# Layer 3's band matrices, stored with the tile index innermost

## The chip, the cores and the metric

The kernel runs on one core of a Trainium2 chip. The metric is the time of one execution on the device, in microseconds (us). A core has TensorE (PE, matrix products; its weight loads are listed apart as PEld), VectorE (DVE), ScalarE (ACT), GpSimd (POOL) and SyncE (SP, which issues the transfers here). SBUF is the on-chip working memory, PSUM the memory that TensorE writes its results to.

## The reference

Four layers act on an input of 16 images of 64 x 64 places and 256 channels, each as `x = x + layer(groupnorm(x))`. The change touches the last one, an involution: a convolution whose 7 x 7 kernel is made anew for each place, from the reduced channels there, and shared by the 16 channels of a group.

```python
def _L3_conv_ref(x, w_reduce, gamma, beta, mean, var, w_span, b_span):
    K = 7; G = 16
    B, H, W, C = x.shape
    r = jnp.einsum('bhwc,cd->bhwd', x, w_reduce)
    r = jax.nn.relu((r - mean) * (gamma / jnp.sqrt(var + BN_EPS)) + beta)
    kgen = jnp.einsum('bhwd,de->bhwe', r, w_span) + b_span
    kgen = kgen.reshape(B, H, W, G, K * K)
    ...
    patches = patches.reshape(B, H, W, K * K, G, Cg)
    out = jnp.einsum('bhwgk,bhwkgc->bhwgc', kgen, patches)
    return out.reshape(B, H, W, C)
```

All numbers are fp32.

## The kernel before

Layers 0 to 2 run first, in stages of their own; layer 3 is the last stage of the program.

Layer 3 cuts a 64 x 64 image into 22 x 8 tiles of 3 rows by 8 columns (`TR`, `TC`; 176 tiles, `NTL`), so a tile has 24 output places (`TILE_OUT`). The places that a tile's outputs look at form a window of 9 x 14 = 126 inputs (`TILE_IN`). For one tile and one group of 16 channels the involution is then one product: the 126 inputs, as rows, times a banded matrix of 126 x 24 that holds the generated kernels at the right rows. The channels are the columns of the stationary operand, the 24 outputs those of the moving one.

`reduced` (L1332) makes the reduced channels `rt` of an image, in a layout by the place within a tile and then by tile (L1360 the products, L1367 their way out of PSUM).

`matrices` (L1375) makes the band matrices of a quarter of the channels (64 channels, 4 groups) of an image. It fills two tiles of memory `w` (name `wm`), one for each pair of groups, `q`. A step `n` makes four output places: for each of them one product (L1393) of the `span` weights, moved by the place's offset within the window, with the 176 tiles' `rt` columns. The results, 4 x 176 floats in each of 128 rows, lie in the PSUM tile `pk`, two places to a bank. They are copied to `wm` with the bias `spanb` added: in 5 of 12 steps by four instructions of ScalarE (L1403, 176 floats each), in 7 of 12 by one of VectorE (L1408, 704 floats). The copy's target is `dst` (L1400). PSUM tiles `pk` are taken from three buffers, so TensorE can be three steps ahead of the copies.

In `wm` the 48 outputs of a pair of groups lie side by side for a tile, and the tiles follow each other: shape [128, 176, 48]. A step's copy writes for each of its four places 176 floats that are 48 floats apart.

`involution7` (L1450) uses them. A turn is two rows of tiles (`k` = 0, 1, eleven tile rows apart) of one quarter of one image: for 8 tile columns `tj`, 2 `k` and 2 `q`, 32 products (L1459). The stationary operand is the window of 32 channels of a pair of groups, from `xw`; the moving operand is that tile's 48 floats of `wm[q]`. The four products of one `tj` write to four different sets of 32 PSUM partitions of `pa`, and so use four column groups of the array. Each product has two instructions in the profile (45,056 for 704 turns). Both of a pair's groups are computed for all of its 32 channels; ScalarE (L1469) and VectorE (L1470) pick the right one by a mask, and POOL (L1477) adds the residual `rx`.

The order is written out by hand, in the loop over `turns` (L1501): 16 images x 4 quarters x 11 turns. In each turn the loads for turns ahead are issued on SP (`xw` four turns ahead, out of six buffers; `rx` two), then `involution7`, then 2 or 3 steps of `matrices` for the quarter that follows (`STEPS`, 24 steps in 11 turns), then now and then a part of `reduced` for the next image. The matrices of the very first quarter are made before the first turn. `wm` has four buffers: two for the quarter in use, two for the one that is being made.

Of the kernel before, what the change touches and what calls it, by code (L numbers as in the profile page):

```python
# [9 lines left out]
F32 = mybir.dt.float32  # L10
# [5 lines left out]
P = 128  # L16
# [13 lines left out]
NTR, NTC = 22, HW // TC  # L30
TILE_IN = (TR + 6) * (TC + 6)
TILE_OUT = TR * TC
# [12 lines left out]
def network(ctx: ExitStack, tc: tile.TileContext, a: dict, out: bass.AP):  # L45
# [139 lines left out]
    with ExitStack() as st:  # L185
# [399 lines left out]
        for n in range(LAST + 16):  # L585
            m, t = divmod(n, NCH)
# [64 lines left out]
    with ExitStack() as st:  # L651
# [24 lines left out]
        with tc.tile_pool(name="s_conv", bufs=1) as pcv:  # L676
# [8 lines left out]
            for dj in range(7):  # L685
                dst = band if dj == 0 else term
# [22 lines left out]
        for n in range(10):  # L709
# [4 lines left out]
                rhs=maps[:, c, :, delta : delta + NB],  # L714
# [5 lines left out]
        m = maps[:, 0, :, 2 : 2 + NB]  # L720
# [18 lines left out]
        with tc.manual_schedule():  # L739
# [25 lines left out]
            for n, (ch, g) in enumerate(steps):  # L765
# [18 lines left out]
                b, k = g * 8, min(8, NI - g * 8)  # L784
# [8 lines left out]
        n = NI * NCH  # L793
# [505 lines left out]
    with ExitStack() as st:  # L1299
        pc = st.enter_context(tc.tile_pool(name="c_const", bufs=1))  # L1300
        wk = st.enter_context(tc.tile_pool(name="c_work", bufs=2))
        wm_p = st.enter_context(tc.tile_pool(name="c_wm", bufs=4))
# [70 lines left out]
        NTL = NTR * NTC  # L1373

        def matrices(i, quarter):  # L1375


            rto = rts[i % 2].rearrange("k a b t u -> k (a b) (t u)")
            wms[i, quarter] = wm = []
            for q in range(2):  # L1380
                w = wm_p.tile([P, NTL, 2 * TILE_OUT], F32, tag="wm", name="wm")
                wm.append(w)
                first = quarter * 4 + q * 2
                for n in range(12):

                    pk = wg.tile([P, 2, CT], F32, tag="wg", name="pk")
                    pkv = pk[:, :, 0 : 2 * NTL].rearrange("p b (m t) -> p b m t", m=2)
                    for m in range(2):
                        for b in range(2):
                            gg, o = divmod(n * 4 + b * 2 + m, TILE_OUT)  # L1390
                            s0 = SPAN - P - (o // TC * (TC + 6) + o % TC)
                            half = slice(b * 64, b * 64 + 64)
                            nc.tensor.matmul(  # L1393
                                pkv[:, b, m],
                                lhsT=span[half, first + gg, s0 : s0 + P],
                                rhs=rto[half, o // 4 * 2 + m, :],
                                start=True, stop=True,
                            )
                    g0 = first * TILE_OUT + n * 4
                    dst = w[:, :, n * 4 : n * 4 + 4].rearrange("p t (b m) -> p b m t", b=2)  # L1400
                    if (q * 12 + n) % 12 in (1, 3, 6, 8, 11):
                        for m in range(4):
                            nc.scalar.activation(  # L1403
                                dst[:, m // 2, m % 2], pkv[:, m // 2, m % 2], AF.Identity,
                                bias=spanb[:, g0 + m : g0 + m + 1],
                            )
                    else:
                        nc.vector.tensor_tensor(  # L1408
                            dst, pkv,
                            spanb[:, g0 : g0 + 4].rearrange("p (b m) -> p b m", b=2).unsqueeze(  # L1410
                                3
                            ).broadcast_to([P, 2, 2, NTL]),
                            ALU.add,
                        )
                    yield
# [3 lines left out]
        NTT = NTR // 2  # L1419
# [30 lines left out]
        def involution7(i, quarter, t, wm, msk, xw, ex, rx):  # L1450


            pa = sm.tile([P, CT], F32, tag="sm", name="pa")
            pav = pa[:, 0 : 2 * TR * HW].rearrange("c (g a w) -> c (g a) w", g=2, w=HW)
            for tj in range(NTC):
                for k in range(2):
                    for q in range(2):
                        p0 = 64 * k + 32 * q
                        nc.tensor.matmul(  # L1459
                            pav[p0 : p0 + 32, :, tj * TC : (tj + 1) * TC],  # L1460
                            lhsT=xw[0:TILE_IN, k, tj, 32 * q : 32 * q + 32],
                            rhs=wm[q][0:TILE_IN, (t + k * NTT) * NTC + tj, :].rearrange(
                                "p (g w) -> p g w", w=TC
                            ),
                            start=True, stop=True,
                        )
            pag = pa[:, 0 : 2 * TR * HW].rearrange("c (g t) -> c g t", g=2)
            h, pr = divmod(quarter, 2)
            nc.scalar.activation(ex, pag[:, 0], AF.Identity, scale=msk[:, pr, h, 0:1])  # L1469
            nc.vector.scalar_tensor_tensor(  # L1470
                ex, pag[:, 1], msk[:, pr, h, 1:2], ex, ALU.mult, ALU.add
            )
            parts = [(slice(0, P), TR * HW)]
            if t == NTT - 1:
                parts = [(slice(0, 64), TR * HW), (slice(64, P), HW)]
            for p, m in parts:
                nc.gpsimd.tensor_tensor(ex[p, 0:m], ex[p, 0:m], rx[p, 0:m], ALU.add)  # L1477
# [19 lines left out]
        for _ in matrices(0, 0):  # L1497
            pass
        done = []
        gap = min(44, (4 * NTT * (NI - 1) - 4) // NCH)  # L1500
        for n, (i, quarter, t) in enumerate(turns):  # L1501
# [17 lines left out]
            if t == 0:  # L1519
                making = iter(())  # L1520
                if n + NTT < len(turns):
                    making = matrices(*turns[n + NTT][:2])
# [17 lines left out]
            if n + 2 in features:  # L1540
                cs[features[n + 2]] = load_reduced(*features[n + 2])
            involution7(i, quarter, t, wms[i, quarter], msk, pats.pop(0), ex[:, t % 2], rx[:, t % 2])
            if n % gap == 2 and n // gap < NCH:
                strip_stores.extend(centred_strips(NI - 1, n // gap, xc, mean))
            for _ in range(STEPS[t]):
                next(making, None)
            if n in features:
                tp, k = features[n]
# [118 lines left out]
```

## Time and profile before

| | us |
|---|---|
| median of 3 runs (8993.86 to 9007.82) | 8996.71 |
| span of the profiled execution, first to last instruction | 8940.3 |
| layer 3: from the first L1393 to the end of the span | 2327.5 |
| layer 3, steady part read below (6640 to 8936) | 2296.0 |

The profiled execution's own time outside of its span isn't on the page; the median of the runs lies 56 us above the span. A page names groups of instructions by line, engine and operation, with what they write and read, how often they ran, and after the first bar their busy time in us and the mean of one in ns; after the second bar stands the idle time of the engine just ahead of them, and what ended it. Busy time is the union of the instructions' spans, so that products running at the same time in several column groups count once. "issue" is a wait for which the profile shows no release. In the list of waits the three numbers are us in total, times, and the longest. In the sums of a stretch the columns are the stretch, its length, then each engine's busy us and number of instructions, the granted TensorE clock as a share of full speed, the busy share of the DMA engines, and GB/s. In the view of one line the durations are least, median and longest in ns.

### The profile page before, as it was taken

The page shows a single profiled execution, that of the slowest core. Times are in us where ns is not written, and L with a number is a line of the kernel's source. Part 1 is how long each engine was busy: PE and PEld are TensorE (multiplying, and loading weights), DVE is VectorE, ACT ScalarE, POOL GpSimd, SP SyncE. Part 2 cuts the span into 40 slices and gives each one's busy share as a digit, 9 for nine tenths or more (in the row PEclk, how much of TensorE's full clock was granted, in tenths as well). Part 3 has the DMA queues.
Part 4 walks back from the last instruction along what each step waited for, and adds up shares of the span by engine and source line. Part 5 has one row for each costly group of instructions (what it writes and reads, how often), then busy time and mean ns, then how long its engine had stood idle before and what let it go on. Part 6 is the DMA issues. An engine that isn't in the chain of part 4 may idle for free. (4 is left out here: it accounts for less than half of the span.)

```text
span 8940.3 us, 213550 instructions
## 1 busy us (share of the span) xinstructions
PE 7239.3 (81%) x84764; PEld 5334.1 (60%) x84764; DVE 6515.6 (73%) x10687; ACT 5059.9 (57%) x12288; POOL 2767.6 (31%) x1962
## 2 busy tenths in 40 slices
PE   7988889888899977477777777777758888888888
PEld 4666666666666653145545444455546666777776
DVE  6676666676666665679999999999945555566665
ACT  3555555555555554666666666665535555566665
POOL 0111111111111110156776776776621111111122
PEclk9999999999999986888888888888879999999999
DMA  6533333333333333767888888887768787888887
GB/s 220 167 121 123 125 123 122 124 123 120 125 109 105 108 110 110 257 205 209 220 225 225 221 227 220 221 230 208 186 165 256 243 252 240 254 258 260 267 260 244
DMA packets 1617992, 1695.63 MB, mean 190 GB/s; under 512 B 855265, under 2 KB 1221170, under 8 KB 1615842
## 3 DMA queue, kind: packets, MB, share of 16 engines
q1 hardware_dynamic: 1616994, 1681.98, 62.1%
q8 instruction: 668, 10.94, 0.5%
q14 instruction: 330, 2.70, 0.1%
HBM read 1234.54 MB, written 469.76 MB: 191 GB/s over the span
## 5 line engine op out<-in xcount | busy, mean ns | idle before, releaser
L287 PE MATMUL pq<-wq,xn 128*128 128x384 f32 x4096 | 1471.9, 503 | 105.3 <-DVE va L303 57.5
L1138 DVE TENSOR_TENSOR pd<-xs,pw 128x576 f32<-128x576 f32 (+15 forms) x3072 | 1438.2, 554 | 10.0 <-PE pw L1092 6.6
L1403 ACT ACTIVATE wm<-pk,spanb 128x176 f32<-128x176 f32 x2560 | 988.6, 543 | 520.8 <-PE pk L1393 500.4
L1408 DVE TENSOR_TENSOR wm<-pk,spanb 128x704 f32<-128x704 f32 x896 | 1174.5, 1354 | 142.5 <-PE pk L1393 130.2
L1393 PE MATMUL pk<-rt,span 64*128 64x176 f32 x12288 | 1199.2, 331 | 96.3 <-issue 44.3
L1149 POOL TENSOR_TENSOR pd<-pd 128x2048 f32<-128x2048 f32 (+2 forms) x384 | 1065.4, 2775 | 296.3 <-DVE pd L1138 276.3
L287 PEld LDWEIGHTS pq<-wq,xn 128*128 128x128 f32 x4096 | 762.7, 195 | 573.8 <-DVE va L303 90.9
L1393 PEld LDWEIGHTS pk<-rt,span 64*128 64x128 f32 x12288 | 982.0, 193 | 196.6 <-issue 67.7
L1477 POOL TENSOR_TENSOR ex<-ex,rx 128x192 f32<-128x192 f32 (+2 forms) x768 | 435.4, 570 | 1855.5 <-DVE ex L1470 1211.0
L1459 PE MATMUL pa<-wm,xw 126*32 126x48 f32 x45056 | 701.4, 211 | 237.2 <-issue 198.3
L1470 DVE SCALAR_TENSOR_TENSOR ex<-pa,msk,ex 128x192 f32<-128x192 f32 x704 | 292.1, 415 | 745.9 <-ACT ex L1469 717.5
L1459 PEld LDWEIGHTS pa<-wm,xw 126*32 126x32 f32 x45056 | 578.1, 112 | 410.7 <-issue 341.1
L1061 PE MATMUL px<-x2p,wis 128*128 128x512 f32 x1024 | 581.4, 711 | 139.6 <-ACT c L1163 99.5
L1108 PEld LDWEIGHTS pt<-ident,pad 128*128 128x128 f32 x4608 | 542.1, 151 | 252.5 <-issue 78.0
L1108 PE MATMUL pt<-ident,pad 128*128 128x128 f32 x4608 | 628.2, 292 | 74.4 <-ACT rt L1085 43.3
L1112 ACT COPY xs<-pt 128x512 f32<-128x512 f32 x1152 | 604.1, 588 | 139.6 <-PE pt L1108 137.4
L456 POOL TENSOR_TENSOR rsy<-ss,mhalf 128x4 f32<-128x4 f32 x128 | 129.8, 1014 | 1704.2 <-DVE ss L454 1704.2
L1284 DVE TENSOR_REDUCE x<-pd 128x512 f32<-128x4608 f32 x128 | 634.1, 4954 | 1.9
L444 PE MATMUL py<-wo,oT 128*128 128x256 f32 x2048 | 472.5, 383 | 28.9 <-DVE va L303 28.9
L1469 ACT ACTIVATE ex<-pa,msk 128x192 f32<-128x192 f32 x704 | 297.6, 423 | 330.7 <-PE pa L1459 229.2
L1082 PE MATMUL pr<-x2r,wrs 128*64 128x512 f32 x512 | 317.7, 754 | 198.3 <-DMA x2r<-x_d 185.2
L303 DVE COPY va<-pq 128x256 f32<-128x256 f32 x512 | 216.6, 423 | 336.2 <-ACT ka L299 315.3
(240 smaller groups left out, 12764.3 us busy)
## 6 DMA issues: line engine op xcount, KB each, us to landing
xw<-strips SPq DMA_DIRECT2D x1408, 256.0 KB
xn<-in_x SPq DMA_DIRECT2D x256, 512.0 KB
x_d<-x SPq DMA_DIRECT2D x256, 512.0 KB
strips<-xc SPq DMA_DIRECT2D x1536, 56.0 KB
xin<-in_x SPq DMA_DIRECT2D x128, 512.0 KB
x<-in_x SPq DMA_DIRECT2D x128, 512.0 KB
xm<-x_d SPq DMA_DIRECT2D x128, 512.0 KB
x<-x_d SPq DMA_DIRECT2D x128, 512.0 KB
```

Source lines behind the costliest of these rows:

```text
L287: nc.tensor.matmul(pq[:, dd, 0:384], lhsT=xn[:, h, tok], rhs=wq[:, h, hf * 384 : (hf + 1) * 384], start=(h == 0), stop=(h == 1),)
L444: nc.tensor.matmul(py[:, q, :], lhsT=oT[hf][:, q * P : (q + 1) * P], rhs=wo[:, hf, :], start=(hf == 0), stop=(hf == 1),)
L1061: nc.tensor.matmul(px, lhsT=w[:, h, fh * P : (fh + 1) * P], rhs=x2[:, h], start=(h == 0), stop=(h == 1),)
L1108: nc.tensor.transpose(pt[:, k, h * P : (h + 1) * P], lines[:, h, rc * 4 + e + k, 2 * j : 2 * j + P], ident,)
L1112: nc.scalar.copy(t[:, e : e + 2, 0:C], pt)
L1138: nc.vector.tensor_tensor(pd[:, :, o - oh * P : o - oh * P + n, :], xs[dj][:, di : di + 4, c0 : c0 + 9 * n].rearrange("p r (f k) -> p r f ...
L1149: nc.gpsimd.tensor_tensor(pd[..., 0:n], pd[..., 0:n], pd[..., n : 2 * n], ALU.add)
L1284: nc.vector.tensor_reduce(x3[:, :, P:C], pd1, AX.X, ALU.add)
L1393: nc.tensor.matmul(pkv[:, b, m], lhsT=span[half, first + gg, s0 : s0 + P], rhs=rto[half, o // 4 * 2 + m, :], start=True, stop=True,)
L1403: nc.scalar.activation(dst[:, m // 2, m % 2], pkv[:, m // 2, m % 2], AF.Identity, bias=spanb[:, g0 + m : g0 + m + 1],)
L1408: nc.vector.tensor_tensor(dst, pkv, spanb[:, g0 : g0 + 4].rearrange("p (b m) -> p b m", b=2).unsqueeze(3).broadcast_to([P, 2, 2, NTL]), AL ...
L1459: nc.tensor.matmul(pav[p0 : p0 + 32, :, tj * TC : (tj + 1) * TC], lhsT=xw[0:TILE_IN, k, tj, 32 * q : 32 * q + 32], rhs=wm[q][0:TILE_IN, (t ...
```

## The change

The tiles `wm` get the shape [128, 48, 176]: the output place first, the tile index innermost. A copy out of PSUM then writes four runs of 176 floats that follow each other, and a product reads its 48 moving floats with a step of 176 floats (704 bytes). The arithmetic, the number and order of instructions on each engine, the buffers and their size in bytes, and the transfers are the same.

```diff
             for q in range(2):
-                w = wm_p.tile([P, NTL, 2 * TILE_OUT], F32, tag="wm", name="wm")
+                w = wm_p.tile([P, 2 * TILE_OUT, NTL], F32, tag="wm", name="wm")
                 wm.append(w)
...
                     g0 = first * TILE_OUT + n * 4
-                    dst = w[:, :, n * 4 : n * 4 + 4].rearrange("p t (b m) -> p b m t", b=2)
+                    dst = w[:, n * 4 : n * 4 + 4, :].rearrange("p (b m) t -> p b m t", b=2)
                     if (q * 12 + n) % 12 in (1, 3, 6, 8, 11):
...
                         nc.tensor.matmul(
                             pav[p0 : p0 + 32, :, tj * TC : (tj + 1) * TC],
                             lhsT=xw[0:TILE_IN, k, tj, 32 * q : 32 * q + 32],
-                            rhs=wm[q][0:TILE_IN, (t + k * NTT) * NTC + tj, :].rearrange(
+                            rhs=wm[q][0:TILE_IN, :, (t + k * NTT) * NTC + tj].rearrange(
                                 "p (g w) -> p g w", w=TC
                             ),
```

## The prediction

> **What bounds the kernel now.** The change touches layer 3 alone, so I read the page first, for the groups of its lines, then the sums of the stretch in which layer 3 runs, then what TensorE waits for there, and last the timeline, for the pace of single instructions.
>
> ```profile
> L1403 ACT ACTIVATE wm<-pk,spanb 128x176 f32<-128x176 f32 x2560 | 988.6, 543 | 520.8 <-PE pk L1393 500.4
> L1408 DVE TENSOR_TENSOR wm<-pk,spanb 128x704 f32<-128x704 f32 x896 | 1174.5, 1354 | 142.5 <-PE pk L1393 130.2
> L1393 PE MATMUL pk<-rt,span 64*128 64x176 f32 x12288 | 1199.2, 331 | 96.3 <-issue 44.3
> ...
> L1459 PE MATMUL pa<-wm,xw 126*32 126x48 f32 x45056 | 701.4, 211 | 237.2 <-issue 198.3
> ```
>
> ```profile
> core 0: us, PE busy (x) PEld busy (x) DVE busy (x) ACT busy (x) POOL busy (x), PEclk, DMA share, GB/s
> 6640.00:8936.00 2296.00, 1947.32 (x58494) 1632.78 (x58490) 1402.01 (x1641) 1359.44 (x3713) 452.62 (x773) 0.96 0.81 253
> ```
>
> TensorE is busy for 1947 of the 2296 us, VectorE and ScalarE for 61% and 59%: TensorE sets the end of this stage. The stage has 704 turns (16 images, 4 quarters, 11 turns), so a turn takes 3.26 us, of which TensorE is idle for about half a microsecond. The waits say why:
>
> ```profile
> PE pa L1459 <- issue: 198.3, 184, 4.0
> PE pk L1393 <- issue: 44.3, 46, 2.7
> PE pk L1393 <- DVE wm L1408: 29.2, 53, 1.5
> PE pa L1459 <- DMA xw<-strips: 21.3, 36, 3.5
> PE pr L1360 <- DMA c<-c_d: 15.6, 12, 3.4
> PE pk L1393 <- ACT wm L1403: 9.6, 29, 0.4
> PE pa L1459 <- ACT rt L1367: 9.5, 34, 0.3
> ```
>
> With the smaller rows of the same answer these come to 342 us. 243 us are "issue": no semaphore explains them. Only about 42 us (29.2 + 9.6 and the small rows 1.0 and 2.6) are waits for the copies that the change makes cheaper. That caps its gain. The timeline gives the paces:
>
> ```profile
> 7704.77 0.47 PE L1393 MATMUL pk<-rt,span 64*128 64x176 f32 x4
> 7705.16 0.90 PE L1360 MATMUL pr<-c,wr 128*64 128x192 f32 x8
> ...
> 7707.09 2.06 PE L1393 MATMUL pk<-rt,span 64*128 64x176 f32 x24
> 7709.08 0.33 PE L1459 MATMUL pa<-wm,xw 126*32 126x48 f32 x11
> ```
>
> ```profile
> 7702.95 0.89 PE L1459 MATMUL pa<-wm,xw 126*32 126x48 f32 x64
> ```
>
> The 64 instructions of a turn at L1459 (32 products, two instructions each) start within 0.89 us less the last one's 0.21 us. Four of them, one for each 32-column group, go at a time, so 16 groups share 0.68 us: 42.5 ns each. A moving column costs 0.83 ns (L287's 384 columns have a median of 486 ns, L1162's 128 one of 273), so this is 48 columns and 2.5 ns. The moving operand, one float each 0.83 ns, is what paces L1459.
>
> **What the Trainium skill says.** "SBUF — State Buffer", Specifications, gives SBUF lines of 16 bytes that need two hits each for full bandwidth; a crossing to a new line pays. The trace of before agrees for writes. Three VectorE operations on 512 floats:
>
> ```profile
> L732 DVE TENSOR_TENSOR r<-r,maps 128x512 f32<-128x512 f32 x1 | 1.0, 1040 | 0.0
> ...
> L731 DVE SCALAR_TENSOR_TENSOR r<-z,az 128x512 f32<-128x512 f32 x1 | 1.0, 1032 | 2.6 <-ACT az L728 2.6
> L726 DVE TENSOR_TENSOR az<-az,z 128x512 f32<-128x512 f32 x1 | 0.7, 693 | 0.0
> ```
>
> L726 is contiguous, L731 writes with a step of 192 bytes, L732 reads and writes so. The step costs (1032 - 693)/512 = 0.66 ns an element, about 1.67 ns in place of the contiguous pace of 1.0; L732's strided reading adds nothing that can be seen beside its writing. For TensorE there is one strided read, on the weight side: L797 loads columns 16 bytes apart, at half clock (0.50 in the sums of its microsecond, below), L1162 contiguous ones.
>
> ```profile
> L797 PEld LDWEIGHTS pt<-ident,fac x4: 197/223/226, 3491.5 to 3492.0; 128*128 128x128 f32 x4
> ```
>
> ```profile
> 3491.50:3492.50 1.00, 0.95 (x4) 0.73 (x4) 0.00 (x0) 0.00 (x0) 0.00 (x0) 0.50 0.00 0
> ```
>
> ```profile
> L1162 PEld LDWEIGHTS pt<-ident,x x1024: 139/142/231, 3891.8 to 6529.0; 128*128 128x128 f32 x171
> ```
>
> Its 223 ns are no more than L1162's longest, 231 ns, which fall where the clock is at half too. At full clock 128 columns take 142 ns and 48 take 103 (L746), 0.49 ns a column; at half clock about twice that. So the weight port takes a new line each 0.8 to 1.0 ns. The same page, Who interferes with whom, gives the moving operand one port of its own; no run shows yet what that port does. "FP8 and Floating Point Precision", TensorE Precision Notes, says that true fp32 takes four passes through the array; the trace shows two instructions for each product, in line with that, but not whether one of them reads a float once or twice. "Runtime: NRT & Kernel Launch", Instruction fetch mechanics, says that instructions come in blocks of 16 KiB (256 of them), fetched while the block before runs, mostly hidden. Here it isn't: 116,984 TensorE records make about 457 blocks in the stage, one each 5.0 us or 1.54 turns. The "issue" waits, 230 of 1.05 us on average, are as many as half of these blocks; I take them for late fetches.
>
> **The change part by part.** No instruction is added, removed or moved, no buffer, wait or DMA changes; each of three groups gets another step.
>
> VectorE's copies, L1408: now 1354 ns for 704 floats written 192 bytes apart. Contiguous, they should be like L726: 160 ns fixed and 1.04 ns an element, 895 ns. That frees 896 x 459 ns = 411 us of VectorE. ScalarE's copies, L1403: 176 floats in 543 ns; L1469 evicts 192 contiguous floats in 423 ns, so 410 ns. That frees 2560 x 133 ns = 340 us of ScalarE. Neither engine is the bound, so what counts is TensorE's 42 us of waiting for them. About half of the blocks end in a late fetch, where a wait saved earlier in the block only makes the fetch later, so I count 22 us; the copies ahead of the first turn, where TensorE goes at their pace (24 steps in 23 us), give another 8. Sum: -30 us. Its bounds are 0 and -60 (all 42 us, and some of the 20 us of waits for L1367, L1469 and L1470, which queue behind these copies).
>
> L1459's 45,056 moving reads: 48 floats that were contiguous (12 lines) become 48 floats 704 bytes apart (48 lines). Before shows no such read. The nearest is L1360, which moves pairs of floats 16 bytes apart, a new line each 1.67 ns in each of two column groups: eight instructions in 0.90 us, a pair of them each 170 ns where 192 columns at 0.83 ns and 2.5 ns make 162.5. So a line each 1.67 ns is hardly punished, but not quite free, as L1393's contiguous pairs are (149 ns against 149.2). From below: a line each 0.83 ns, about what the weight port takes, keeps the group at 42.5 ns and costs nothing. From above for one column group alone: a line each 1.67 ns makes 80 + 2.5 ns a group. I take this upper value: it is the pace of strided writes, what the skill's rule of two hits leads to if a float is read once for each of two passes, and L1360 looks like a stream just at that limit. Cost: 16 x 40 ns = 0.64 us a turn, 704 x 0.64 = 451 us.
>
> Not all of it reaches the end. TensorE's work for a block of 1.54 turns grows by 0.98 us, so late fetches of 1.05 us mean shrink; if their spread is about exponential, exp(-0.98/1.05) = 39% remains, and 243 - 95 = 148 us come back. Of the other 99 us of waits (copies, loads, evictions) I take 75 as gone, since everything TensorE waits for is earlier against it. 451 - 148 - 75 = +228 us. What is late next is L1459 itself. Against the profiled span of 8940.3 us that is 9168 us; the runs' median lies 56 us above the span (8996.7), so 9225 us.
>
> **The rivals.**
>
> Free reading (not slower): the moving port takes a line each 0.83 ns like the weight port, and four column groups don't get in each other's way. Then only the copies count: 8997 - 30 = 8967 us, between 8937 and 8997. For it: L797. Against it: L1360's 7 ns.
>
> One port for four streams (much slower): four column groups read different columns at once. Contiguous, they ask for 4 lines each 3.33 ns, or 1.2 lines a nanosecond; L1360's two groups ask for the same 1.2, and already lose a little. If that is a common limit, 192 lines a group take 160 ns: 16 x 120 ns x 704 = 1352 us more, less the whole 342 us of idle time: 10,007 us or more. Against it: nothing shows that the four share anything.
>
> Copies no faster: PSUM would limit them. L1287 reads 512 floats from PSUM in 684 ns, the pace of L726, so I give it no share of its own; it would take the 30 us off either case.
>
> **How the numbers follow.** Halved reading 0.44, free reading 0.39, one port 0.17. The forecast's own range runs from 9105 (451 us less all 342 us of idle time) to 9420 (only the waits for copies gone). The whole range takes in free reading from 8935 and ends at 9440; the common port is left out. 0.2%, or 18 us, is about what this measurement can tell from no change: free reading is faster by more than that in three cases of four (0.30), else the same (0.09); with a little of halved reading that is fully hidden, same is 0.10 and slower 0.60.
>
> **What would show it.** Right: L1459's 64 instructions spread over some 1.5 us in place of 0.89, in groups of about 82 ns; its busy time near 1150 us; "issue" waits well under 243 us; L1408 near 895 ns and L1403 near 410. The forecast is wrong if the groups keep 42.5 ns (then TensorE's 42 us decide), or if they take 160 ns. Ends of matrix instructions are modelled, so their starts are to be read, not their durations. If the groups slow down but the "issue" waits stay, the cover that I counted on is not there, and the time is near 9400.

## The result, and the profile after

The changed kernel takes 9023.77 us (median of 13 runs, 9012.17 to 9036.17) against 8997.75 for the one before (13 runs, 8989.15 to 9019.41). The ratio is 1.0027, with an interval of 1.0019 to 1.0035: slower by about 26 us. The forecast was slower, but by 228.

The page of the changed kernel has the two copies where the forecast put them, and TensorE's two groups far from where they were:

```profile
L1393 PE MATMUL pk<-rt,span 64*128 64x176 f32 x12288 | 1137.0, 323 | 26.2 <-DVE wm L1408 9.2
...
L1459 PE MATMUL pa<-wm,xw 126*32 126x48 f32 x45056 | 1109.6, 264 | 43.8 <-issue 43.1
...
L1403 ACT ACTIVATE wm<-pk,spanb 128x176 f32<-128x176 f32 x2560 | 834.2, 409 | 494.8 <-PE pk L1393 471.8
...
L1408 DVE TENSOR_TENSOR wm<-pk,spanb 128x704 f32<-128x704 f32 x896 | 789.3, 888 | 175.2 <-PE pk L1393 162.1
```

L1408 went from 1354 to 888 ns (895 forecast), L1403 from 543 to 409 (410 forecast). L1459 is busy for 408 us more. Its idle time fell from 237 us to 44, and L1393, which was not touched, is busy for 62 us less. The timeline of TensorE shows the new pace (start, length, both in us); below it stands the line of before that follows the turn at 7702.95 shown in the prediction:

```profile
7702.37 2.06 PE L1393 MATMUL pk<-rt,span 64*128 64x176 f32 x24
7704.36 1.59 PE L1459 MATMUL pa<-wm,xw 126*32 126x48 f32 x64
7705.88 1.46 PE L1393 MATMUL pk<-rt,span 64*128 64x176 f32 x16
```

```profile
7703.77 1.46 PE L1393 MATMUL pk<-rt,span 64*128 64x176 f32 x16
```

The 64 instructions of a turn take 1.57 to 1.59 us where they took 0.89. Starts alone, which are not modelled, say nearly the same: from the first instruction of a turn to the L1393 that follows, 1.52 us (7704.36 to 7705.88) where it was 0.82 (7702.95 to 7703.77). From the start of one instruction to that of the fourth after it, so from group to group, the median of all turns is 85 ns, where it was 43. L1393 keeps its pace. Over 704 turns 0.68 us make 479 us that TensorE has to stream longer, and the kernel is 26 us slower. So the question is what took up the rest. The sums of layer 3, from the first L1459 to the end, and the largest waits after:

```profile
6646.40:9018.30 2371.90, 2293.57 (x58656) 1982.10 (x58654) 1047.32 (x1646) 1274.34 (x3723) 455.93 (x776) 0.99 0.80 245
```

```profile
PE pa L1459 <- issue: 35.3, 40, 2.8
PE pk L1393 <- DVE wm L1408: 9.2, 14, 1.0
PE pk L1393 <- issue: 7.6, 13, 1.1
```

TensorE is busy for 97% of this stretch. It has 78 us of idle time left, and its clock is granted at 0.99 where it was 0.96.

### The profile page after: what moved, and what is told of

The parts are those of the page before. It is cut to its first block, busy times and chain, and to the rows that moved or that the text cites. A ratio compares the mean times of both kernels' runs of the same rounds, so it can differ in the third digit from the quotient of the medians.

```text
span 9018.3 us, 213550 instructions
## 1 busy us (share of the span) xinstructions
PE 7583.4 (84%) x84764; PEld 5682.1 (63%) x84764; DVE 6154.1 (68%) x10687; ACT 4972.4 (55%) x12288; POOL 2768.2 (31%) x1962
## 4 chain that ended last, share of the span: by engine, by line
PE 43%; DVE 18%; DMA 13%; ACT 10%; issue 9%; POOL 4%; SPq 3%; DVEq 0%; POOLq 0%; ACTq 0%
PE pa L1459 12%; PE pk L1393 11%; PE pq L287 7%; DVE pd L1138 6%; PE py L444 4%; DMA c_d<-c 3%; DMA xn<-in_x 3%; DMA x<-x_d 2%; DVE x L1284 2%; ACT sq L453 2%; SPq L1241 2%; PE pr L1360 2%; PE po L407 2%; PE px L1061 1%; ACT y L459 1%
## 5 line engine op out<-in xcount | busy, mean ns | idle before, releaser
L1393 PE MATMUL pk<-rt,span 64*128 64x176 f32 x12288 | 1137.0, 323 | 26.2 <-DVE wm L1408 9.2
L1459 PE MATMUL pa<-wm,xw 126*32 126x48 f32 x45056 | 1109.6, 264 | 43.8 <-issue 43.1
L1403 ACT ACTIVATE wm<-pk,spanb 128x176 f32<-128x176 f32 x2560 | 834.2, 409 | 494.8 <-PE pk L1393 471.8
L1459 PEld LDWEIGHTS pa<-wm,xw 126*32 126x32 f32 x45056 | 964.2, 125 | 188.3 <-issue 163.3
L1393 PEld LDWEIGHTS pk<-rt,span 64*128 64x128 f32 x12288 | 940.4, 187 | 150.9 <-issue 34.3
L1408 DVE TENSOR_TENSOR wm<-pk,spanb 128x704 f32<-128x704 f32 x896 | 789.3, 888 | 175.2 <-PE pk L1393 162.1
L1061 PEld LDWEIGHTS px<-x2p,wis 128*128 128x128 f32 x1024 | 209.7, 220 | 398.0 <-issue 210.5
```

Of the source, the lines that this page charges most:

```text
L1061: nc.tensor.matmul(px, lhsT=w[:, h, fh * P : (fh + 1) * P], rhs=x2[:, h], start=(h == 0), stop=(h == 1),)
L1393: nc.tensor.matmul(pkv[:, b, m], lhsT=span[half, first + gg, s0 : s0 + P], rhs=rto[half, o // 4 * 2 + m, :], start=True, stop=True,)
L1403: nc.scalar.activation(dst[:, m // 2, m % 2], pkv[:, m // 2, m % 2], AF.Identity, bias=spanb[:, g0 + m : g0 + m + 1],)
L1408: nc.vector.tensor_tensor(dst, pkv, spanb[:, g0 : g0 + 4].rearrange("p (b m) -> p b m", b=2).unsqueeze(3).broadcast_to([P, 2, 2, NTL]), AL ...
L1459: nc.tensor.matmul(pav[p0 : p0 + 32, :, tj * TC : (tj + 1) * TC], lhsT=xw[0:TILE_IN, k, tj, 32 * q : 32 * q + 32], rhs=wm[q][0:TILE_IN, :, ...
```

## The experiments

The experiments ran in three groups, each on a chip of its own (e1 to e4, e5 to e8, e9 to e11), and the kernel before had medians of 8950.69, 8954.46 and 8999.3 us there. So each ratio is to the kernel before in its own group. Even so, the changed kernel's ratio is 1.0027 in the result and 1.0052 in e5, with intervals that don't meet: a ratio of one group can differ by some 20 us from that of another.

**e1: the kernel before once more**, unchanged.

> The kernel before once more, for a second profile of it. The first profile's span, 8940 us, lay below all 13 timed runs (8989 to 9019), and the span of the changed kernel, 9018 us, lay 2 us below the time of its own run; so 56 us between span and median, on which the forecast was built, looks like a fast execution and not like time outside of the span. If so: span and time of one run within 5 us of each other, the span near 8995, and TensorE's idle time in layer 3 nearer 390 us than 342. If the 56 us are outside of the span: a span near 8940 again.

Its run took 8963.75 us and its span is 8961.7: 2 us lie outside of the span, as for the changed kernel (9018.3 and 9020.18). So the 56 us of the forecast were no time outside of the span: the execution that was profiled for it must have been a faster one. The span is not near 8995, as was expected: this chip's runs of the kernel lie lower. TensorE's idle time is 359 us, between the 342 of the first profile and the 390 expected. The sums of its layer 3, and its largest waits:

```profile
6643.20:8961.70 2318.50, 1959.13 (x58655) 1645.03 (x58652) 1404.53 (x1646) 1363.21 (x3723) 454.30 (x776) 0.96 0.80 251
```

```profile
PE pa L1459 <- issue: 191.9, 181, 4.0
PE pk L1393 <- issue: 46.9, 44, 3.6
```

**e2: the strided reads alone.** Copies as before; the products read what lies there as if it were laid out by the change.

```diff
-                            rhs=wm[q][0:TILE_IN, (t + k * NTT) * NTC + tj, :].rearrange(
+                            rhs=wm[q].rearrange("p t o -> p (t o)").rearrange(
+                                "p (o t) -> p o t", t=NTL
+                            )[0:TILE_IN, :, (t + k * NTT) * NTC + tj].rearrange(
```

> Copies as before (48 floats apart, slow), products read with the step of 704 bytes; so the values that the products read are not those of their tile. Theory P (TensorE had slack before because something else, not TensorE, paced the stage, and the slower reads filled it): L1459's groups at 84 ns, TensorE nearly without idle time, time 0 to 40 us above the changed kernel, since VectorE's and ScalarE's slower copies are still under TensorE's time. Theory C (the cheap copies gave back a large part of the 485 us that the reads cost): 100 us or more above the changed kernel.

1.0077 of before (1.0056 to 1.0098), or 69 us slower; groups at 85 ns. The changed kernel had 1.0027, and 1.0052 when run again in e5, so by the ratios the cheap copies are worth some 22 to 45 us where the reads are slow; the lower figure is not clear of noise (the intervals of e2 and e5 meet). By the traces it is 14 to 25 us: layer 3 takes 2385.8 us here, 2371.9 in the result's trace and 2360.8 in e5. That is within Theory P's 40 us or just over it, and far from Theory C's 100.

**e3: both halves cheap.** Two neighbouring tiles lie innermost, so that a copy writes runs of two floats and a product reads with a step of two. (The copies' target is rearranged to match; that part is left out here.)

```diff
-                w = wm_p.tile([P, NTL, 2 * TILE_OUT], F32, tag="wm", name="wm")
+                w = wm_p.tile([P, NTL // 2, 2 * TILE_OUT, 2], F32, tag="wm", name="wm")
...
-                            rhs=wm[q][0:TILE_IN, (t + k * NTT) * NTC + tj, :].rearrange(
-                                "p (g w) -> p g w", w=TC
-                            ),
+                            rhs=wm[q][
+                                0:TILE_IN, ((t + k * NTT) * NTC + tj) // 2, :, tj % 2
+                            ].rearrange("p (g w) -> p g w", w=TC),
```

> wm as [128, 88, 48, 2]: two neighbouring tiles innermost. Copies write runs of 2 floats, products read with a step of 2 floats (8 bytes), so each 16-byte line is hit twice by both. If two hits of a line are enough: L1408 near 890 ns, L1403 near 410 ns, L1459's groups at 42.5 ns: both halves cheap. Theory P: even so only 0 to 40 us under before, because TensorE doesn't set the pace. Theory C: 100 us or more under before. If two hits aren't enough, L1408 stays above 1100 ns or the groups go above 50 ns.

All three prices came down: L1408 888 ns, L1403 418, L1459's groups 45 ns in the median (43 before). The time is that of before, 0.9998 (0.9988 to 1.0007). The first fence has the groups of instructions, the second TensorE's waits, both of e3:

```profile
L1403 ACT ACTIVATE wm<-pk,spanb 128x176 f32<-128x176 f32 x2560 | 839.8, 418 | 539.7 <-PE pk L1393 520.8 <-PE pa L1459 15.0 <-issue 3.2
L1408 DVE TENSOR_TENSOR wm<-pk,spanb 128x704 f32<-128x704 f32 x896 | 789.2, 888 | 247.4 <-PE pk L1393 238.1 <-PE pa L1459 7.6
```

```profile
PE pa L1459 <- issue: 221.5, 187, 4.2
PE pk L1393 <- issue: 55.6, 58, 3.1
PE pr L1360 <- DMA c<-c_d: 28.7, 14, 5.7
PE pk L1393 <- DVE wm L1408: 9.2, 13, 1.1
```

L1393's waits for VectorE's copies went from 29.7 us in e1 to 9.2, those for ScalarE's from 10.1 to 3.9. The "issue" waits went from 239 us (191.9 + 46.9, e1) to 277. What the copies no longer kept TensorE waiting for, it waited for elsewhere. The reads are not quite free here: L1459 is busy for 719 us, 17 more than in e1. So what the copies alone are worth beside fast reads can be some us above nothing; together the two halves gave nothing.

**e4: half the instructions at L1459.** The kernel before, where one product covers two neighbouring tiles.

```diff
-            for tj in range(NTC):
+            for tj in range(0, NTC, 2):
...
-                            pav[p0 : p0 + 32, :, tj * TC : (tj + 1) * TC],
+                            pav[p0 : p0 + 32, :, tj * TC : (tj + 2) * TC].rearrange(
+                                "c g (t w) -> c g t w", w=TC
+                            ),
```

> The kernel before, but one product covers two neighbouring tiles (96 moving floats, the window of the left one for both; so the right tile's values are not the reference's). TensorE streams as many columns, with 32 instruction pairs at L1459 a turn in place of 64, and some 104 in place of 168 in all; the transfers of data are the same. Theory F (the pace of before is set by the fetching of TensorE's instructions, one 16 KiB block each 5.0 us, 1.5 turns): blocks then hold 2.5 turns, late fetches vanish, 150 to 300 us under before. Theory D (the data transfers, 250 GB/s, set the pace): within 40 us of before, with TensorE's idle time under DMA names in place of issue.

0.9839 of before (0.9819 to 0.9860): 144 us faster, just short of Theory F's 150 and far from Theory D's 40. The waits of TensorE:

```profile
PE pr L1360 <- DMA c<-c_d: 87.2, 52, 4.9
PE pa L1459 <- DMA xw<-strips: 78.7, 133, 2.2
PE pk L1393 <- DVE wm L1408: 64.9, 90, 3.5
```

There is not one "issue" wait of TensorE in layer 3, where e1 has 239 us of them. The instruction queue moved 493 blocks in the whole program in place of 668. So the "issue" waits do come with the number of TensorE's instructions. That they are late fetches can be read in e1's trace, from its single records. Of its "issue" waits 174 are longer than 0.5 us. Nine in ten of these end 1.24 to 1.58 us after the last packet of the instruction queue; for moments picked at random that range is 0.3 to 5.8 us. And from one such wait to the next there are 256, 512 or 768 records of products and weight loads in most cases: one, two or three blocks. Theory D is there too, as what is late next: 166 us of waits for `c` and `xw`, with the DMA engines at 0.84 in place of 0.80. The sums of layer 3 of e4:

```profile
6618.70:8800.80 2182.10, 1922.27 (x36128) 1544.18 (x36126) 1390.70 (x1646) 1350.71 (x3723) 451.17 (x776) 0.96 0.84 265
```

**e5 and e6: the change again, and the change with half the instructions.** e5 is the changed kernel. e6 has e4's edit on it; its moving operand covers both tiles with the step of 704 bytes:

```diff
-                            rhs=wm[q][0:TILE_IN, :, (t + k * NTT) * NTC + tj].rearrange(
-                                "p (g w) -> p g w", w=TC
-                            ),
+                            rhs=wm[q][
+                                0:TILE_IN, :, (t + k * NTT) * NTC + tj : (t + k * NTT) * NTC + tj + 2
+                            ].rearrange("p (g w) t -> p g t w", w=TC),
```

> The changed kernel once more, beside the next three on one chip. Both theories: 1.002 to 1.005 of before, L1459's groups at 84 ns, TensorE idle for less than 100 us of layer 3.

> The changed kernel with one product for two neighbouring tiles, as in e4 (96 moving floats at the step of 704 bytes, the left tile's window for both; the right tile's values are not the reference's). Theory F (late instruction fetches were the slack that the slower reads filled): e4 has no late fetches, so here the slower reads find less to fill: TensorE sets the pace, the time is within 40 us of the changed kernel, and so 100 to 180 us above e4 (0.984 of before), four times what the change costs in the kernel itself. Theory R (the slack is general, from waits of every kind, and fills up whatever its source): 20 to 70 us above e4.

e5: 1.0052 of before (1.0036 to 1.0068), groups at 85 ns. e6: 0.9946 (0.9931 to 0.9961). Sums of layer 3 of e5, then of e6:

```profile
6628.10:8988.90 2360.80, 2290.45 (x58656) 1981.95 (x58653) 1047.53 (x1646) 1271.54 (x3723) 456.00 (x776) 1.00 0.79 246
```

```profile
6624.70:8907.00 2282.30, 2253.26 (x36126) 1785.22 (x36124) 1045.82 (x1646) 1272.05 (x3723) 456.19 (x776) 1.00 0.81 253
```

The same reads cost 0.0107 in e6 against e4, about 96 us, where they cost 26 to 47 in the kernel itself. The two ran on different chips, but their traces say the same: layer 3 is 100 us longer in e6, against 42 from e1 to e5. Neither theory's number held: F had 100 to 180 and a time near the changed kernel's (e6 is 95 us below), R at most 70. The price about doubles where the late fetches are gone, but other waits fill as well: e4 had 260 us of idle time (2182.1 us less 1922.3 busy), e6 has 29.

**e7 and e8: half the window traffic**, before and changed. Only the windows of `k` = 0 are loaded, and both halves use them.

```diff
-            for k in range(2):
+            for k in range(1):
                 t0 = (t + k * NTT) * TR * (TC + 6)
...
-                            lhsT=xw[0:TILE_IN, k, tj, 32 * q : 32 * q + 32],
+                            lhsT=xw[0:TILE_IN, 0, tj, 32 * q : 32 * q + 32],
```

> The kernel before, with the windows of the lower half alone loaded and used for both halves (256 KB less for each turn, of some 840; the upper half's values are not the reference's). TensorE has the same instructions and streams. If instruction fetches are late because they stand behind the data transfers: issue waits of TensorE under 120 us (239 in e1), 80 to 250 us under before. If a fetch takes its time whatever the traffic: issue waits near 240 us still, at most 60 us under before (waits for windows alone).

> The same with the changed kernel. TensorE is already busy for 97% of its layer 3, so less traffic gives at most 60 us in either theory; if e7 falls by 80 us or more, the price of the change becomes e8 less e7, 80 to 300 us.

e7: 0.9757 of before (0.9740 to 0.9773), 217 us faster. e8: 0.9976 (0.9966 to 0.9986), 21 us faster than before and 68 under e5, a little over the 60 expected. The same reads now cost 0.0219, about 196 us. Sums of layer 3 of e7:

```profile
6624.50:8745.50 2121.00, 1893.40 (x58654) 1600.57 (x58652) 1403.28 (x1646) 1348.84 (x3723) 456.52 (x776) 0.98 0.64 188
```

and its first waits:

```profile
PE pa L1459 <- issue: 144.5, 143, 4.6
PE pk L1393 <- issue: 22.6, 33, 1.6
```

The "issue" waits came down with the traffic from 239 us to 167, neither under 120 nor near 240. So the traffic has a part in late fetches. How large it is stays open: the waits for `xw` went as well, and e3 showed that "issue" waits grow when other waits go.

**e9: a new line for each float, but only 16 bytes on.** Runs of four tiles innermost; the other lines are as in e3, with 4 for 2.

```diff
-                w = wm_p.tile([P, NTL, 2 * TILE_OUT], F32, tag="wm", name="wm")
+                w = wm_p.tile([P, NTL // 4, 2 * TILE_OUT, 4], F32, tag="wm", name="wm")
```

> wm as [128, 44, 48, 4]: copies write runs of 4 floats, products read with a step of 16 bytes, so that each moving float lies in a line of its own, but next to the one before. If the price of the strided reads is one of lines (each new line costs a column group 1.67 ns): L1459's groups at 82 to 86 ns, time like the changed kernel, 1.002 to 1.007 of before. If it is one of distance (704 bytes apart, and with it the banks that they fall into): groups at 42.5 to 50 ns, time like before.

1.0044 of before (1.0030 to 1.0058). The groups have 89 ns in the median, slightly over what was expected. A step of 16 bytes costs what a step of 704 does; a step of 8 bytes (e3) costs next to nothing. So the price depends on whether two floats of a stream fall in the same 16 bytes, not on how far apart they lie.

**e10 and e11: one column group at a time**, changed and before.

```diff
-            for tj in range(NTC):
-                for k in range(2):
-                    for q in range(2):
+            for k, q, tj in [(k, q, tj) for k in range(2) for q in range(2) for tj in range(NTC)]:
+                if True:
+                    if True:
```

> The changed kernel, with the loop over the tiles innermost: 16 instructions in a row go to one column group, and the streams no longer overlap. The same products, the same result. If the 84 ns are a limit of one stream: 80 to 88 ns from each instruction at L1459 to the next, about 5.3 us for the 64 of a turn. If four streams share one port (a line each 0.42 ns): a stream alone isn't held up, 42 to 50 ns each, about 2.8 us for the 64.

> The kernel before in the same order, as the measure for e10: 42.5 ns from one instruction at L1459 to the next in both theories.

Single runs of 10952 and 9604 us. A turn's 64 instructions in e10, then in e11:

```profile
7606.79 4.49 PE L1459 MATMUL pa<-wm,xw 126*32 126x48 f32 x64
```

```profile
7603.58 2.49 PE L1459 MATMUL pa<-wm,xw 126*32 126x48 f32 x64
```

The median from one instruction to the next is 83 ns in e10 and 42 in e11. The totals are below 64 times that, because streams still overlap where the column group changes, but their ratio is 1.8. Single runs are enough for a difference of this size. A stream that goes nearly alone is held up as much as four at once, so the limit belongs to a stream and isn't shared.

## Why the prediction was wrong

**The reads: right.** "A line each 1.67 ns" gave 82.5 ns a group and 451 us; measured are 85 ns and 479. It was one of two bounds, chosen on thin evidence, and it held. e3 and e9 show that it is a price of lines and not of distance, e10 that the limit is a stream's own. The rival of free reading falls with that, and so does the common port: four streams at once take 85 ns, not 160. What spoke for free reading, L797's weight loads, was no evidence, for they ran at half clock. There the moving operand shows hardly any price either: in the stretches at half clock contiguous groups take 80 ns in the median (1157 groups of three traces: before, e1, e7), and strided ones 86, as at full clock (95 groups of five: after, e2, e5, e8, e9).

**The copies: their durations right, their worth wrong.** 888 and 409 ns stand against 895 and 410. The -30 us that they were to give where reading costs nothing did not show in e3 (0.9998), whose reads cost a little. I had argued that late fetches eat half of what a saved wait gives; in e3 the "issue" waits grew by 38 us, more than the 27 us that L1393's waits for copies lost. Beside slow reads, where few fetches are late, the copies give 14 to 45 us (e2 against both runs of the change). In the sum of +228 they had no term of their own; their waits were among the 75 us.

**The cover: this step failed.** "451 - 148 - 75 = +228 us" takes the longer reads as 451 us of busy time and lets 223 us of waits take up a part. From e1 to e5 TensorE's busy time in layer 3 grew by 331 us and its idle time fell by 289: +42 us. So of the 186 us by which the forecast is off against this pair, 120 lie in busy time that did not come, and 66 in waits that shrank more than was forecast.

The waits: idle time fell from 359 us to 70. Of the 239 us of "issue" waits 45 are left (19%, forecast 39%), and of the 106 us of other waits 16 (the remainder of the idle time is pauses too short for the list of waits). The exponential spread was too cautious, and the trace of before could have said so: each of its 230 "issue" waits shortened by the forecast's 0.98 us leaves 71 us, or 29%. Why still fewer are left is not shown.

**The busy time was taken as it stood, clock and all.** TensorE's busy time grew from 1959 to 2290 us, though L1459 has 479 us more to stream. L1459's own busy time grew by 406, and L1393 lost 65 us (1203.3 to 1137.9) with nothing changed in it, while the mean granted clock of the stage rose from 0.96 to 1.00. The clock is lost in short stretches at half speed. One of them, from e1: TensorE's timeline, and the sums of the stretch.

```profile
6936.39 0.37 PE L1459 MATMUL pa<-wm,xw 126*32 126x48 f32 x4 [2.81 <-DMA xw<-strips]
...
6938.35 3.31 PE L1393 MATMUL pk<-rt,span 64*128 64x176 f32 x20
```

```profile
6935.90:6942.70 6.80, 6.15 (x140) 5.49 (x144) 2.73 (x3) 1.95 (x5) 1.48 (x3) 0.50 0.88 268
```

Here 20 instructions of L1393 take 3.31 us; at full clock 24 take 2.06. In e1 TensorE is busy for 169 us of layer 3 at half clock, in e5 for 13. So most of these stretches went with the waits, and work that had been slow became fast: half of the difference, an estimated 75 us, is busy time that the kernel got back. The forecast's own lines showed the 0.96, and it took all durations as if the clock stood still. This term was put at nothing without a reason.

It is about half of the 148 us between 479 and 331. The rest fits the tails that waits leave: the last instruction before a wait counts as busy to its modelled end, 206 ns at L1459, though the next group could have started after 43. From the start of the last instruction to its end these tails add up to 120 us in e1 and 40 in e5. That part is an estimate too, and nothing was tried on it.

Long waits and the low clock go together: 36 of the 38 stretches at half clock in e1 begin within 4 us of the end of a wait of more than 1 us or in it, and such places make up less than a third of the stage. The means agree in direction only: idle 359, 260, 228 and 70 us in e1, e4, e7 and e5, clock 0.96, 0.96, 0.98 and 1.00. That the one causes the other was not tried.

So 42 us between e1 and e5 stand beside the 47 us of e5's ratio and the 26 of the result. That the slack, and not something in the change, made it cheap is shown by taking slack away: the same reads cost 26 to 47 us where TensorE idled for 359, 96 where it idled for 260, and 196 where it idled for 228. The direction that was forecast is right, but what is left is a small rest of large terms.

**The range's lower bound** for this case, 9105, came from 451 - 342 = 109 us, all idle time of the trace. It left out the clock and the tails. Besides, the 342 us were those of a faster execution than the ones that took 8997 us (e1); no trace of one of these is on record, so how much they idled isn't known.

## What to carry to other kernels

An engine that is busy for 85% of a stage need not be what paces it, and then its busy share prices nothing: making its work longer fills its waits first, and making its partners faster can merely move the waits. Before pricing an edit there, ask what paces the stage, and try it by taking that away: here halving TensorE's instructions at one line gave 144 us, and making both copies cheaper with the reads nearly as fast as before gave nothing. A granted clock under 1.0 in the stage can be slack, too: here an estimated 75 us came back as the waits went.

## What the runs showed of the hardware that was not expected

A moving fp32 operand read with a step of 8 bytes streams nearly as fast as a contiguous one (45 ns against 43 for a group of 48 columns), and with 16 bytes or 704 about half as fast (89 and 85 ns); with 704 this holds for one stream (83 ns) as for four. The strided pace does not follow TensorE's clock: where that was halved, strided groups took 86 ns still, and contiguous ones 80, so nearly the whole price of the stride is gone there. ScalarE's and VectorE's writes behave alike: runs of two floats, 384 bytes apart, cost nearly what contiguous ones cost (888 and 418 ns against 888 and 409), single floats 1354 and 543. So in this kernel a layout with two of the inner index side by side serves both sides. It takes 384 us of busy time off VectorE and 149 off ScalarE, and no time off the kernel, because the stage waits for TensorE's instructions and, behind them, for its transfers.
